# Rotary embedding in an attention slot: one 128-partition sine product with its halves swapped by SBUF transfers, and q and k projected two slots ahead

## The chip, the cores and the metric

The kernel runs on one core of one Trainium2 chip. Its time is device microseconds; three runs gave 617.77, 617.89 and 618.55 us, median 617.89. One further execution was taken with a profile. The engines are named as in the profile: PE (TensorE), with PEld for its weight loads, DVE (VectorE), ACT (ScalarE), POOL (GpSimd) and SP (SyncE, which issues all transfers of this kernel).

## What is computed

Two layers on x of 2 x 512 x 256, each an attention part and a feed-forward part, with norms between. The change touches the attention of the first layer only. Cut to what matters:

```python
D_MODEL, N_HEADS, D_K = 256, 16, 128

def rope(x):                                  # x: batch, position, head, 128
    cos, sin = ...                            # by position and frequency
    x_rot = concatenate([-x[..., 64:], x[..., :64]], axis=-1)
    return x * cos + x_rot * sin

q = rope((x @ wq.T + bq).reshape(b, s, N_HEADS, D_K))
k = rope((x @ wk.T + bk).reshape(b, s, N_HEADS, D_K))
v = (x @ wv.T + bv).reshape(b, s, N_HEADS, D_K)
attn = softmax(where(causal, -inf, einsum('bihd,bjhd->bhij', q, k) / sqrt(D_K)))
o = einsum('bhij,bjhd->bihd', attn, v).reshape(b, s, N_HEADS * D_K)
out = o @ wo.T + bo + residual
```

Then follow a feed-forward part with four-bit weights (gelu), a linear attention, and a feed-forward part whose weights are looked up in a table of 16 values (silu).

## The kernel before

All is float32. The first layer's attention is a loop over 32 slots (2 batches x 16 heads), `slot(i)`, with two more slots to drain. The order of every engine's instructions is the order in which the program writes them; nothing reorders them later. Two helpers record each instruction, which is why most rows of the profile bear the same line: L183 for DVE, ACT and POOL, L165 for transfers, L282 for matmuls. A matmul of 128 output rows is written as two of 64 rows (`halved`).

Head dimension lies on the partitions: q and k of a head are tiles of 128 x 512 (head dimension x positions). `projection(kind, i)` (L874) makes one of them. Two input chunks are multiplied into a PSUM bank `ps_mm`. Then the rotation: `a = (ps + bias) * cos`, for q as one DVE instruction, for k as an ACT instruction that adds the bias and a POOL product with cos. The half-swapped part is made straight into place by two DVE products of 64 partitions each, from the high half of PSUM to the low half of `r` and the other way (L913, L916). At the end POOL adds, `to = a + r` (L924), and the tile is qT or kT. The tiles `ra` (a) and `rr` (r) come from the pool `qk` with two buffers per tag, taken in turn by q and k; Tq and Tk also had two buffers each.

In slot i the program writes, in this order:

1. scores of head i (L1184 to L1212): PE, on the banks ps_s and ps_t. Into parts of these banks, which no score matmul starts, ACT has copied a piece of the mask a slot earlier (`prepare`, L993). DVE adds the mask and takes minima (`p<-ps_s,mask`, `mn`), ACT takes the exponentials with their sums.
2. `catch_up()`: one step of dequantising four-bit weights, if there is one: a cast on ACT, five DVE bit operations, or one DVE product of 128 x 1024. New weights are asked for in even slots from 2 on (`dequantised`, three transfers on SP), so bit operations fall into odd slots' middle and the product to their end.
3. `look_up(1)`: one of 32 terms of a table look-up: DVE writes `scratch`, POOL adds it into `wg`.
4. projections of q and k of head i+1, with the rotation; between the two, DVE's reciprocal of the sums, `rs`. Both ends `a + r` follow on POOL.
5. ACT multiplies the four blocks of p by rs.
6. PE: the output projection of head i-2 (`ps_o<-wo,oT`), then attention times v of head i-1 (`ps_t<-pT,v`), after which ACT prepares the next mask copies and evacuates oT.
7. DVE transposes the four blocks of p in 32 x 32 pieces (`turned`), and SP issues four transfers that bring them to the tile `pT` (one buffer), which step 6 of the next slot reads.
8. PE: values of a later group (`ps_mm<-wv,xTv`), evacuated by ACT; steps of norm chains that are due (`poll`); another catch_up.

The banks are taken in turn per tag (`bank`): ps_mm has two, used by q, k and v.

A small planner (`Times`, `Engine`) keeps modelled start and end times of what is written. It decides where to put `fills`: pieces of another table look-up on DVE, from slot 17 on, written when the model sees DVE waiting. The model knows tiles by the name of each allocation.

Of the kernel before, what the change touches and what calls it, by code (L numbers as in the profile page):

```python
# [10 lines left out]
F32 = mybir.dt.float32  # L11
# [5 lines left out]
AF = mybir.ActivationFunctionType  # L17
ALU = mybir.AluOpType

P = 128  # L20
HALF = P // 2
B = 2
S = 512
D = 256
NT = S // P
NK = D // P
# [15 lines left out]
NEG = -1e30  # L42
SWAPPED = (1, 2)
WARM = 9
REST = INTER - (NO - 1) * P


# [53 lines left out]
class Engine:  # L101
# [48 lines left out]
    def __getattr__(self, name):  # L150
        write = getattr(self.engine, name)

        def written(*args, **more):
            out = args[0] if args else more["out"]
            outs = [a for a in (out, more.get("accum_out")) if Times.on_chip(a)]
            ins = [
                a
                for a in (*args[1:], *(a for k, a in more.items() if k not in ("out", "accum_out")))
                if Times.on_chip(a)
            ]  # L160
            start = self.times.start(self.who, outs, ins)
            if name == "dma_start":
                self.busy = max(self.busy, start) + (0.8 if len(outs) + len(ins) == 2 else 0.45)
                self.times.add("DMA", self.busy + 3.4, outs, ins)
                return write(*args, **more)  # L165
            if self.fills and not self.filling:
                self.fill(start - 0.1)
            start = max(start, self.busy)
            psum = any("PS" in str(a.space) for a in (*outs, *ins))
            if self.other and not psum and name in Engine.HELD:  # L170
                for a, b in self.other.spans:
                    if a <= start < b:
                        start = b
            kind = dict(more)
            if name == "activation":
                kind["func"] = args[2]
            if ALU.pow in args:
                kind["pow"] = True
            n = max(math.prod(a.shape[1:]) for a in (*outs, *ins))
            self.busy = start + self.cost(name, n, kind, psum)  # L180
            self.spans.append((start, self.busy))
            self.times.add(self.who, self.busy, outs, ins)
            return write(*args, **more)  # L183

        return written
# [5 lines left out]
def sandwich_kernel(  # L191
# [26 lines left out]
    nc = tc.nc  # L218
# [10 lines left out]
    vector, scalar = Engine("DVE", nc.vector, times), Engine("ACT", nc.scalar, times)  # L229
    pool, sync = Engine("POOL", nc.gpsimd, times), Engine("SP", nc.sync, times)  # L230
# [3 lines left out]
    def bank(tag):  # L234
        tile = psum.tile([P, 512], F32, tag=tag, name=f"ps_{tag}")
        used = banks.setdefault(tag, deque(maxlen=2))
        if len(used) == 2:
            times.floor[tile.name] = times.end(used[0])
        used.append(tile.name)
        return tile  # L240
# [36 lines left out]
    def matmul(out, lhsT, rhs, start, stop, beside=False, **more):  # L277
        m = lhsT.shape[-1]
        step = HALF if halved[0] else P
        for at in range(0, m, step):  # L280
            part = slice(at, min(at + step, m))
            nc.tensor.matmul(out[part], lhsT=lhsT[:, part], rhs=rhs, start=start, stop=stop, **more)  # L282
        now[0] = max(now[0], times.start("PE", [out], [lhsT, rhs]))
        if not beside:
            now[0] += (math.prod(rhs.shape[1:]) / 0.6 + 5) / 1e3
        times.add("PE", now[0], [out], [lhsT, rhs])
# [19 lines left out]
    cos_sb = const.tile([P, S], F32, name="cos_sb")  # L306
    sin_sb = const.tile([P, S], F32, name="sin_sb")
# [9 lines left out]
    FULL = NO - 1  # L317
    wg = w1.tile([P, NK, FULL * P + 64 + REST], F32, name="wg")
    wu = w1.tile([P, NK, FULL * P], F32, name="wu")
# [17 lines left out]
    def chunk(t, kc):  # L337

        return t[:, :, kc].rearrange("p a j t -> p j a t")
# [193 lines left out]
    with ExitStack() as at:  # L533
        wp = at.enter_context(tc.tile_pool(name="wp", bufs=2))
        vp = at.enter_context(tc.tile_pool(name="vp", bufs=2))
        qk = at.enter_context(tc.tile_pool(name="qk", bufs=2))
# [40 lines left out]
        def warm_up(n):  # L577
            for _ in range(n):
                nc.tensor.matmul(warm[:, :P], lhsT=units, rhs=units, start=True, stop=True)  # L579

        warm_up(WARM)

# [4 lines left out]
        xT0 = [  # L587
            ac.tile([P, NK, S] if b == 0 else [P, 4, NK, NT, 32], F32, name=f"xT0_{b}") for b in range(B)
        ]
# [256 lines left out]
        for u in range(NU):  # L846
            for src, sc, name, to in ((gate_p, gate_s, "g", wg_u), (up_p, up_s, "u", wu_u)):
                w = fw.tile([P, 2, UNIT], F32, name=f"w{name}{u}")
                jobs.append((src, sc, u, name, w))
                to.append(w)  # L850
        for u in range(NU):
            w = fw.tile([P, 2, UNIT], F32, name=f"wd{u}")
# [9 lines left out]
        NS = B * NH  # L862
        qT, kT, vs, pT, ps_p, yb = {}, {}, {}, {}, {}, {}
# [10 lines left out]
        def projection(kind, i, tag="mm"):  # L874


            b, h = divmod(i, NH)
            gg, hh = divmod(i, HG)
            w = wts[kind, gg]
            bias = col(kind, h)  # L880
            a = qk.tile([P, S], F32, tag="ra", name="ra")
            r = qk.tile([P, S], F32, tag="rr", name="rr")
            to = qk.tile([P, S], F32, tag=f"T{kind}", name=f"{kind}T")
            lo, hi = slice(0, 64), slice(64, 128)


            for cs in [slice(0, TU), slice(TU, S)] if i == 0 else [slice(0, S)]:
                ps = bank(tag)
                first_half = i == 0 and cs.start == 0
                tiles = [slice(0, P), slice(P, TU)] if first_half and kind == "q" else [cs]  # L890
                for n, (ts, kc) in enumerate((ts, kc) for ts in tiles for kc in range(NK)):
                    matmul(
                        ps[:, ts],
                        w[:, hh, kc, :],
                        chunk(xT0[b], kc) if b else xT0[b][:, kc, ts],
                        kc == 0,
                        kc == NK - 1,
                    )
                    if first_half and (kind, n) in (("q", 1), ("k", 0)):
                        yield  # L900
                yield
                def by_scalar():
                    scalar.activation(a[:, cs], ps[:, cs], AF.Identity, bias=bias)
                    pool.tensor_mul(a[:, cs], a[:, cs], cos_sb[:, cs])


                if i and (kind == "k") == (i > 1):
                    by_scalar()
                elif not first_half:
                    vector.scalar_tensor_tensor(  # L910
                        a[:, cs], ps[:, cs], bias, cos_sb[:, cs], ALU.add, ALU.mult
                    )
                vector.scalar_tensor_tensor(  # L913
                    r[lo, cs], ps[hi, cs], bias[hi], sin_sb[hi, cs], ALU.add, ALU.mult
                )
                vector.scalar_tensor_tensor(  # L916
                    r[hi, cs], ps[lo, cs], bias[lo], sin_sb[lo, cs], ALU.add, ALU.mult
                )
                if first_half:
                    by_scalar()  # L920
            yield
            if (kind, i) == ("k", 1):
                inverted(0)
            (pool if i > 1 or kind == "q" else vector).tensor_add(to, a, r)  # L924
            (qT if kind == "q" else kT)[i] = to
# [215 lines left out]
        begun = {}  # L1141

        def started(kind, i):
            work = projection(kind, i)
            next(work)
            return work


        def slot(i):
            b, h = divmod(i, NH)  # L1150
# [65 lines left out]
            else:  # L1216
                assert not terms
            turning = []
            for kind in "qk":
                if kind == "q" and i in (0, 2, 3):  # L1220
                    pass
                elif i + 1 < NS:
                    turning.append(begun.pop((kind, i + 1), None) or started(kind, i + 1))
                    next(turning[-1])
                elif i <= NS:
                    next(main)
                    next(main)
                if kind == "q" and jobs and i % 2 == 0 and i >= 2:
                    dequantised(*jobs.popleft())
                if kind == "q" and i and now_in:  # L1230
                    inverted(i)
            for work in turning:
                next(work, None)
            if now_in:
                p, _ = ps_p[i]
                for it in reversed(range(NT)):
                    pi = p[:, p_at[it] : p_at[it] + (it + 1) * P]
                    scalar.mul(pi, pi, rs[i][:, it : it + 1])
# [37 lines left out]
        for rows, cs, base in (  # L1276
# [5 lines left out]
                out=mask[rows, cs],  # L1282
                in_=mask[rows, cs],
# [19 lines left out]
        main = ffn_hidden(0)  # L1303
# [122 lines left out]
    def silu_hidden(u):  # L1426
# [12 lines left out]
        for o in range(0, NO, 2):  # L1439
# [15 lines left out]
            else:  # L1455
# [3 lines left out]
                vector.tensor_mul(  # L1459
                    hT[:REST, o + 1, :], si[:REST, TU:], pg[64 : 64 + REST, TU:]  # L1460
                )
# [177 lines left out]
```

## Time and profile before

| what | value |
|---|---|
| median of three runs | 617.89 us |
| profiled execution, span | 616.7 us (616.669) |
| one attention slot, scores to scores (173.96 to 184.94 to 195.92) | 10.98 us |
| the same two slots, DVE busy | 9.60 and 8.23 us |
| the same two slots, ACT busy; POOL busy | 7.11 and 6.59; 5.54 and 5.54 us |
| the same two slots, mean busy share of the 16 DMA engines | 0.51 and 0.67 |
| from 600 to 610 us, and from 610 to the end: PE busy | 10.00 of 10.00, and 2.00 of 6.60 us |

Attention takes the first 350 us or so of the span; the feed-forward parts and the linear attention fill the rest. The span is from the first instruction to the last. An odd slot such as the one from 173.96 carries a step of dequantising, the even one after it does not. Columns of the timeline lines below: start and duration in us, engine, line, operation, output<-inputs, shape, number of instructions merged into the line, and in brackets the idle time of the engine ahead of it with what ended it. Pages of waits name a releaser that is inferred from semaphores.

Of the transfers the page says, with size each and median us from issue to landing:

```profile
pT<-turned SPq DMA_DIRECT2D x128, 208.0 KB, 3.9
wq<-in_wq SPq DMA_DIRECT2D x15, 256.0 KB, 4.2
sc_g<-in_gate_s SPq DMA_DIRECT2D x8, 128.0 KB, 4.2
```

SP's own timeline over one slot's pT transfers and the loads behind them:

```profile
184.22 3.17 SPq L165 DMA_DIRECT2D pT<-turned  x4
187.43 0.59 SPq L165 DMA_DIRECT2D wv<-in_wv  x1
188.07 1.12 SPq L165 DMA_DIRECT2D wo<-in_wo  x1
189.30 0.38 SPq L165 DMA_DIRECT2D pk_u<-in_up_p  x1
189.78 1.50 SPq L165 DMA_DIRECT2D sc_u<-in_up_s  x2
```

### The profile page before, as it was taken

To read this page: it belongs to the slowest core of one execution; us is meant where nothing else is said; L and a number is where in the kernel's file an instruction comes from. 1 tells how busy PE (TensorE), PEld (TensorE's weight loads), DVE (VectorE), ACT (ScalarE), POOL (GpSimd) and SP (SyncE) were. 2 spreads that over 40 slices of the span, in tenths; PEclk is the share of its full clock that TensorE was granted. 3 is DMA by queue.
4 is the path that set the end of the run, shared out by engine and by line. 5 is a ranking of instruction groups with operands and counts; after the bars stand their busy time and mean duration, and the time that the engine had idled before them with its cause. 6 is when DMAs were issued, how large, how long until landed. Compare 5 with 4: busy or idle time off the path is not lost.

```text
span 616.7 us, 13347 instructions
## 1 busy us (share of the span) xinstructions
PE 611.1 (99%) x4968; PEld 470.2 (76%) x4968; DVE 486.2 (79%) x1169; ACT 309.3 (50%) x716; POOL 277.1 (45%) x346
## 2 busy tenths in 40 slices
PE   9999999999999999999999999999999999999996
PEld 7455556566676776767777899999999999996665
DVE  7989988887887999989899789869986751562963
ACT  6657776775666657676566651232324223325210
POOL 5355657454453575855667300350261350161531
PEclk9999999999999999999999999999999999999999
DMA  8477474765647547556552340211001000001010
GB/s 228 137 186 211 107 199 125 171 168 144 158 127 177 168 116 191 152 142 178 113 141 60 84 104 26 98 35 35 1 8 31 1 18 18 1 2 35 19 53 18
DMA packets 44463, 61.43 MB, mean 100 GB/s; under 512 B 5232, under 2 KB 32368, under 8 KB 44400
## 3 DMA queue, kind: packets, MB, share of 16 engines
q1 hardware_dynamic: 44400, 60.59, 38.0%
q8 instruction: 39, 0.64, 0.4%
q14 instruction: 24, 0.20, 0.1%
HBM read 28.59 MB, written 1.05 MB: 48 GB/s over the span
## 4 chain that ended last, share of the span: by engine, by line
PE 98%; DVE 1%; issue 0%; POOL 0%; DVEq 0%
PE ps_mm L282 40%; PE ps_o L282 22%; PE ps_s L282 21%; PE ps_t L282 14%; PE ps_o L579 1%; DVE x L183 0%; DVE p L183 0%; DVE rr L183 0%; DVE ra L183 0%; DVE centred L183 0%; POOL rstd L183 0%; DVE wg L183 0%; PE ps_t L289 0%; DVE st L183 0%; DVE st_last L183 0%
## 5 line engine op out<-in xcount | busy, mean ns | idle before, releaser
L183 DVE SCALAR_TENSOR_TENSOR rr<-ps_mm,cols_sb,sin_sb 64x512 f32<-64x512 f32 (+1 forms) x126 | 93.4, 741 | 3.6 <-PE ps_mm L282 0.7
L183 POOL TENSOR_TENSOR wg<-wg,scratch 128x752 f32<-128x752 f32 x30 | 53.8, 1794 | 89.3 <-DVE scratch L183 86.9
L282 PE MATMUL ps_mm<-xT,wg 128*64 128x256 f32 (+1 forms) x704 | 89.4, 379 | 0.0
L282 PE MATMUL ps_s<-xT,wu 128*64 128x256 f32 x672 | 85.4, 379 | 0.0
L183 ACT ACTIVATE p<-p,mn 128x512 f32<-128x512 f32 (+3 forms) x128 | 70.3, 550 | 27.6 <-DVE mn L183 27.6
L282 PE MATMUL ps_o<-wd,hT 128*64 128x256 f32 (+1 forms) x704 | 77.2, 375 | 0.0
L282 PE MATMUL ps_t<-pT,v 128*64 128x256 f32 (+3 forms) x512 | 76.1, 432 | 0.0
L282 PEld LDWEIGHTS ps_mm<-xT,wg 128*64 128x64 f32 (+1 forms) x704 | 71.7, 137 | 5.5 <-ACT si L183 0.4
L282 PEld LDWEIGHTS ps_o<-wd,hT 128*64 128x64 f32 x704 | 68.9, 137 | 6.2
L282 PEld LDWEIGHTS ps_s<-xT,wu 128*64 128x64 f32 x672 | 69.5, 137 | 4.5 <-DVE hT L183 0.3
L282 PEld LDWEIGHTS ps_t<-pT,v 128*64 128x64 f32 x512 | 49.7, 137 | 27.1 <-issue 19.0
L183 ACT ACTIVATE p<-p,rs 128x512 f32<-128x512 f32 (+3 forms) x128 | 61.4, 551 | 11.2 <-DVE rs L183 9.3
L282 PEld LDWEIGHTS ps_o<-wo,oT 128*64 128x64 f32 x512 | 49.9, 137 | 17.8 <-issue 13.3
L282 PE MATMUL ps_o<-wo,oT 128*64 128x256 f32 x512 | 62.5, 379 | 0.0
L282 PE MATMUL ps_mm<-xT,wq 128*64 128x512 f32 (+2 forms) x256 | 60.5, 577 | 0.1
L282 PE MATMUL ps_mm<-xT,wk 128*64 128x512 f32 x248 | 60.0, 592 | 0.0
L183 POOL TENSOR_TENSOR ra<-ra,cos_sb 128x512 f32<-128x512 f32 (+1 forms) x33 | 41.1, 1245 | 40.2 <-ACT ra L183 38.4
L282 PE MATMUL ps_s<-kT,qT 128*64 128x64 f32 (+5 forms) x384 | 57.0, 424 | 0.0
L282 PE MATMUL ps_mm<-wv,xTv 128*64 128x256 f32 x464 | 56.4, 379 | 0.0
L183 DVE STREAM_TRANSPOSE turned<-p 128x512 f32<-128x512 f32 (+3 forms) x128 | 54.1, 480 | 1.2 <-ACT p L183 0.2
L183 ACT ACTIVATE ln<-x,shift,rstd 128x256 f32<-128x256 f32 x22 | 13.3, 607 | 79.0 <-POOL shift L183 78.2
L282 PEld LDWEIGHTS ps_s<-kT,qT 128*64 128x64 f32 x384 | 34.6, 137 | 23.9 <-issue 11.6
(161 smaller groups left out, 965.3 us busy)
## 6 DMA issues: line engine op xcount, KB each, us to landing
pT<-turned SPq DMA_DIRECT2D x128, 208.0 KB, 3.9
wo<-in_wo SPq DMA_DIRECT2D x17, 256.0 KB, 4.2
wv<-in_wv SPq DMA_DIRECT2D x16, 256.0 KB, 4.2
wq<-in_wq SPq DMA_DIRECT2D x15, 256.0 KB, 4.2
wk<-in_wk SPq DMA_DIRECT2D x15, 256.0 KB, 4.0
xT<-tr SPq DMA_DIRECT2D x48, 64.0 KB, 2.1
pk_g<-in_gate_p SPq DMA_DIRECT2D x4, 256.0 KB, 4.6
sc_g<-in_gate_s SPq DMA_DIRECT2D x8, 128.0 KB, 4.2
```

What stands on the lines that cost most here:

```text
L183: return write(*args, **more)
L282: nc.tensor.matmul(out[part], lhsT=lhsT[:, part], rhs=rhs, start=start, stop=stop, **more)
L579: nc.tensor.matmul(warm[:, :P], lhsT=units, rhs=units, start=True, stop=True)
```

## The change

From head 5 on (`FROM`) the rotation is written in another way. The sine product becomes one DVE instruction of 128 partitions into a new tile `y`, and SP swaps its halves into `r` by two transfers of 64 partitions. q and k of head i+2 are projected, rotated and swapped in slot i, instead of those of head i+1; the final sum `a + r` of head i+1 is written in slot i just before. The tiles Tq and Tk get a third buffer; `ra`, `rr` and the new `ry` have two. Slot 3 projects both head 4 and head 5. In slots 30 and 31, where no head is left, pieces of the first feed-forward part (`main`) take the place of projections. The planner's rule for transfers changes: a transfer is taken to wait for its inputs, and for earlier transfers into its output. The program is built with a smaller scratch area for transfers (1024).

```diff
+FROM = 5
...
             if name == "dma_start":
+                start = max(self.times.start(self.who, [], ins), self.times.start("DMA", outs, []))
...
-            to = qk.tile([P, S], F32, tag=f"T{kind}", name=f"{kind}T")
+            to = qk.tile([P, S], F32, tag=f"T{kind}", name=f"{kind}T", bufs=3)
             lo, hi = slice(0, 64), slice(64, 128)
+
+            if i >= FROM:
+                ps = bank(tag)
+                for kc in range(NK):
+                    matmul(
+                        ps,
+                        w[:, hh, kc, :],
+                        chunk(xT0[b], kc) if b else xT0[b][:, kc, :],
+                        kc == 0,
+                        kc == NK - 1,
+                    )
+                yield
+                y = qk.tile([P, S], F32, tag="ry", name="ry")
+                if kind == "q":
+                    vector.scalar_tensor_tensor(a, ps, bias, cos_sb, ALU.add, ALU.mult)
+                else:
+                    scalar.activation(a, ps, AF.Identity, bias=bias)
+                    pool.tensor_mul(a, a, cos_sb)
+                vector.scalar_tensor_tensor(y, ps, bias, sin_sb, ALU.add, ALU.mult)
+                for half, other in ((lo, hi), (hi, lo)):
+                    sync.dma_start(out=r[half], in_=y[other])
+                yield
+                pool.tensor_add(to, a, r)
+                (qT if kind == "q" else kT)[i] = to
+                return
...
             turning = []
+            if FROM <= i + 1 < NS:
+                for kind in "qk":
+                    next(begun.pop((kind, i + 1)), None)
             for kind in "qk":
                 if kind == "q" and i in (0, 2, 3):
                     pass
+                elif i + 1 >= FROM:
+                    if i + 2 < NS:
+                        begun[kind, i + 2] = started(kind, i + 2)
+                        next(begun[kind, i + 2])
+                    elif i <= NS:
+                        next(main)
+                        if i + 2 > NS:
+                            next(main)
...
             for work in turning:
                 next(work, None)
+            if i == FROM - 2:
+                for kind in "qk":
+                    begun[kind, FROM] = started(kind, FROM)
+                    next(begun[kind, FROM])
...
-    nc = bacc.Bacc("TRN2", target_bir_lowering=False, num_devices=1)
+    nc = bacc.Bacc("TRN2", target_bir_lowering=False, num_devices=1, dynamic_dma_scratch_size=1024)
```

The constants of the kernel: NS = 32 slots, NK = 2 input chunks, P = 128 partitions, S = 512 positions; `begun` holds projections that are under way, `started` makes one and runs its matmuls, each further `next` runs it to its next `yield`.

## The prediction, made before the changed kernel was run

> **What bounds the kernel now.** I read the busy shares first, then the granted clock by slices, then the chain of work that ended last.
>
> ```profile
> PE 611.1 (99%) x4968; PEld 470.2 (76%) x4968; DVE 486.2 (79%) x1169; ACT 309.3 (50%) x716; POOL 277.1 (45%) x346
> ...
> PEclk9999999999999999999999999999999999999999
> ...
> PE 98%; DVE 1%; issue 0%; POOL 0%; DVEq 0%
> ```
>
> TensorE holds 99% of the span, at full clock, and 98% of the last chain. "Busy" can hide waiting, so I looked at the order of time in one attention slot (slot 15, an odd one), TensorE first:
>
> ```profile
> 173.96 1.78 PE L282 MATMUL ps_s<-kT,qT 128*64 128x512 f32 x12
> ...
> 181.06 2.38 PE L282 MATMUL ps_t<-pT,v 128*64 128x512 f32 x16
> ...
> 184.94 0.60 PE L282 MATMUL ps_s<-kT,qT 128*64 128x512 f32 x2
> ```
>
> The slot lasts 10.98 us from scores to scores, and so does the next (184.94 to 195.92), though VectorE has 9.60 us of work in the one and 8.23 in the other (busy time by stage). A period that ignores VectorE's load is TensorE's own work. So in attention nothing outside TensorE sets the time, and taking work from VectorE can gain almost nothing: the change adds and removes no matmul, and 616.67 - 611.1 = 5.6 us of TensorE idleness lies at the two ends (0.76 before the first matmul, 4.6 in the last 6.6). What can move is upwards only: how close are the other engines to making TensorE wait? VectorE, GpSimd and ScalarE in slot 15:
>
> ```profile
> 177.87 0.61 DVE L183 TENSOR_SCALAR scratch<-scratch,lut_sb 128x752 f32<-128x752 int32 x1
> 178.39 0.75 DVE L183 SCALAR_TENSOR_TENSOR ra<-ps_mm,cols_sb,cos_sb 128x512 f32<-128x512 f32 x1
> 179.15 1.51 DVE L183 SCALAR_TENSOR_TENSOR rr<-ps_mm,cols_sb,sin_sb 64x512 f32<-64x512 f32 x2
> 180.70 0.18 DVE L183 RECIPROCAL rs<-sm 128x4 f32<-128x4 f32 x1
> 180.91 1.51 DVE L183 SCALAR_TENSOR_TENSOR rr<-ps_mm,cols_sb,sin_sb 64x512 f32<-64x512 f32 x2
> 182.46 1.69 DVE L183 STREAM_TRANSPOSE turned<-p 128x512 f32<-128x512 f32 x4
> ```
>
> ```profile
> 178.56 1.79 POOL L183 TENSOR_TENSOR wg<-wg,scratch 128x752 f32<-128x752 f32 x1 [5.35 <-DVE scratch L183]
> 180.44 1.28 POOL L183 TENSOR_TENSOR ra<-ra,cos_sb 128x512 f32<-128x512 f32 x1
> 181.67 1.28 POOL L183 TENSOR_TENSOR qT<-ra,rr 128x512 f32<-128x512 f32 x1
> 182.91 1.28 POOL L183 TENSOR_TENSOR kT<-ra,rr 128x512 f32<-128x512 f32 x1
> ```
>
> ```profile
> 179.67 0.69 ACT L183 ACTIVATE ra<-ps_mm,cols_sb 128x512 f32<-128x512 f32 x1 [1.52 <-PE ps_mm L282]
> 180.91 1.92 ACT L183 ACTIVATE p<-p,rs 128x512 f32<-128x512 f32 x4 [0.55 <-DVE rs L183]
> 182.86 0.21 ACT L183 COPY ps_s<-mask 64x64 f32<-64x64 f32 x1
> ```
>
> The reader is to see three things. The copy of the mask into ps_s ends at 183.07; the scores at 184.94 need it, so it has 1.87 us to spare. GpSimd sits idle 5.35 us until the look-up product `scratch` is ready, then does wg, ra, qT, kT; kT ends 0.75 us before its scores. And the transposes end at 184.15; their four transfers to pT take 3.17 us to issue and the last lands near 190.85, against TensorE's use of pT at 192.03: 1.2 us to spare.
>
> **The change part by part.** Below, t is time from the slot's first score matmul (173.96 is t = 0).
>
> *Sine products.* Two 64x512 products of 0.75 us become one 128x512. Its nearest row is the cosine product, 128x512 from the same bank, 0.75. So VectorE is rid of 2 x 0.76 = 1.5 us a slot, 27 heads (5 to 31), some 41 us in all. On the path: nothing, TensorE covers it.
>
> *Swap by transfers.* Four more transfers of 128 KB a slot on SP's queue. They land in time: a 64-partition 128 KB transfer (sc_g) takes 4.2 us to land, so q's, issued by 8.9, are there at 13.1 and k's, issued by 12.1 at the latest, at 16.3; the sums that need them come in the next slot, after t = 17 and 18. [...]
>
> *The wait that is added.* The final sum of head i+1 (`to = a + r` on GpSimd) is now issued in slot i's middle, behind the look-up sum wg, and right after it the cosine product of head i+2 is written. Tiles "ra" have two buffers for q and k in turn, so q of head i+2 takes the buffer that q of head i+1 is still to be read from. VectorE's `ra` for q must wait for GpSimd's qT sum, ScalarE's `ra` for k for its kT sum. Before, the buffers were read a slot earlier, and these sums came after all of it. Behind VectorE's wait stand y of q, rs, y of k and the four transposes (and with them pT); behind ScalarE's stand the four p products, the mask copies, oT and v.
>
> Odd slot with look-up and dequantising (7 to 25 but 17, and 5: ten slots): scratch ends at t = 4.52, wg 4.60 to 6.39, qT to 7.67, kT to 8.91 (sums start 1.24 apart), ScalarE's ra +0.06 and 0.69 to 9.66, the p products 1.92 to 11.58, the copy 0.03 + 0.21 to 11.82, and 0.08 until the scores start: 11.90, against 10.98. Late by 0.92. Hand-overs of 0.03 to 0.08 are those seen between engines in these rows. Ten slots: 9.2, and with 0.03 of lag in each slot that follows (below), 9.5 us.
>
> Even slot: scratch ends at 3.46 (188.40), all the rest alike: 10.84. No wait, but 0.14 of margin.
>
> *VectorE's lag into the next slot.* In the odd slot VectorE starts ra at 7.73, y(q) ends 9.24, y(k) waits for ScalarE's ra and ends 10.47, transposes 12.20, the dequantised weights (1.20, 1.12 of it after the transposes' recorded end) 13.24. The next slot's score reductions could start at 11.90 + 1.17 = 13.07. So any further work at the end of an odd slot makes the next slot late by about its length, since idle time spent in the new wait cannot be used by what is queued behind. From the rows (statistics 0.42, aggregate 0.18, add 0.52, transpose 0.43, h sum 0.68) this is 1.40 in slot 5, 0.85 in 7, 2.24 in 19, 0.85 in 21, 2.24 in 23, 0.85 in 25: 8.4. Ends of even slots (1.26 in slot 4, 1.2 in 18 and 22, with a fill of 0.43 in each of the latter two) exceed their 1.09 of room and give 1.25; the second look-ups of slots 26 to 29 some 0.9. Together 10.6. At the low end these are hidden (0), if the norm work lands where GpSimd makes VectorE wait anyway.
>
> *SP's queue.* In even slots up to 22 the packed weights and scales (0.38 + 1.50 to 2.4 us of issue; I take 2.0) stand between q's swap and k's. q's y ends at t = 8.18, two issues of 0.6 (the 256 KB loads' row, 0.59; pT's own transfers take 0.55 to 1.17) to 9.45, weights to 11.45, k's to 12.65: only then can pT go, instead of 11.2. Its last landing, 6.63 after its first issue, is t = 19.28; TensorE wants it at 10.98 + 7.10 = 18.08. The odd slot that follows stops 1.2 at pT and lasts 8.30 + 3.88 = 12.18 instead of 11.90. Ten slots x 0.28 = 2.8, less where slots are longer anyway: 2.5 us. If the last landing takes 8.2 (the worst in this trace after the transposes, median 6.7), every slot stops there and the whole becomes 35 to 38; if SP keeps up, 0.
>
> Sum: 9.5 + 10.6 + 2.5 = 22.6 us on the profiled 616.67, that is 639.3. The runs' median, 617.89, lies 1.22 above the profiled span; with that, 640.5.
>
> *Third buffers for qT and kT, less scratch for DMA, the two earlier projections in slot 3, feed-forward pieces in slots 30 and 31.* The same matmuls in another place; TensorE's count is unchanged and the pieces moved cover the same dependent work. Nothing; if a piece of cover is missed there, one slot's wait, about 1 us.
>
> *Clock.* It is 1.00 in all stages but the last 6.6 us, where TensorE works 2.0 us and it reads 0.84. My waits are at most 2.4 us in a slot of 11 to 13, so I count nothing. [...]
>
> **Rivals.**
> *Not slower: the wait is covered.* If GpSimd's sums ran before the look-up sum is ready (q's operands have landed by t = 2.1), VectorE would not wait, transposes end 1.5 us earlier than now, and every slot stays 10.98: 617.9. It decides at t = 4.0: the qT sum must end before that. Against it: the code issues the look-up before the sums, and each engine's rows follow issue order. Chance 0.05; a gain over 0.2% has nothing to come from but the idle ends: 0.01 of it.
> *Chain alone.* The wait is there, but the lag at the slots' ends is absorbed: 9.5 to 14, so 627 to 632. For it: VectorE has 1.5 us less to do. Chance 0.17.
> *pT becomes the bound.* 4 x 128 KB a slot more on engines that are 0.51 to 0.67 busy there, ahead of pT in the queue: landing 7.7 to 8.2 gives 30 to 38, so 648 to 656. For it: landings up to 8.2 occur already. Against: the median is 6.7 with the present load. Chance 0.2.
>
> **How the numbers follow.** Forecast (632 to 648, most likely 640.5) 0.55; chain alone 0.17; pT bound 0.2; covered 0.05; further out 0.03. Range 626 to 656, from the chain alone to the late landing. A measurement of this kernel can tell about 0.2% (1.2 us) from no change: slower 0.95, same 0.04, faster 0.01.
>
> **What would show it.** Right: in the profile after, VectorE's `ra` stands idle some 3 us on GpSimd's qT; ScalarE's `ra` on kT; score matmuls wait on ScalarE's mask copy; slots alternate near 11 and 12 us; sine products of 128x512 at 0.75. Wrong: slots still 10.98 (the wait is covered), TensorE waiting at ps_t for pT in every slot (the transfers bound it), or a clock below 1.00 in attention.

## The result, and the profile after

The changed kernel takes 643.56 us (median of 4 runs, 643.17 to 644.24), the kernel before beside it 618.22 (617.77 to 618.7): a ratio of 1.0413, 95% interval 1.0398 to 1.0428. The forecast was 640.5, in a range of 626 to 656. The profiled execution has a span of 642.3 us, 25.6 more than the 616.67 before.

First the busy shares, TensorE's row of the slices and the chain of the changed kernel's page, as before (the helpers' lines are now L185, L167 and L284):

```profile
span 642.3 us, 13490 instructions
PE 616.1 (96%) x4968; PEld 397.1 (62%) x4968; DVE 436.9 (68%) x1115; ACT 304.8 (47%) x716; POOL 276.0 (43%) x346
...
PE   9999899999999998899799999999999999999996
...
PE 54%; issue 17%; POOL 13%; ACT 5%; DMA 4%; DVE 4%; SPq 2%; POOLq 0%; DVEq 0%
```

VectorE is rid of 49 us (486.2 before): by its groups 40.7 of them are the sine products (93.4 before, 40.3 + 12.4 after). But the chain of waits, which was TensorE to 98%, is TensorE to 54% now; GpSimd has 13% of it. Where they meet is in the view of waits (engine, tile and line, what ended the idle time, us in all, times, longest):

```profile
ACT ra L185 <- POOL kT L185: 104.1, 27, 4.7
...
DVE ra L185 <- POOL qT L185: 78.3, 25, 3.2
...
PE ps_t L284 <- DMA pT<-turned: 16.3, 13, 2.2
...
PE ps_s L284 <- ACT ps_s L185: 1.7, 3, 0.6
```

The two rows of `ra` are new; the kernel before has neither wait. VectorE stands 3.1 us in each of 25 slots, and ScalarE 3.9 in each of 27, in front of a product into `ra` until GpSimd has made a final sum. But the rows of TensorE, the engine that counts, say that what it waits for last is mostly not ScalarE's copy of the mask (1.7 us) but pT's transfers (16.3). Slot 15, engine by engine (start, duration, the operation, the idle time before it and its releaser; the slot's scores start at 188.51, and t counts from the start of a slot's scores, as in the forecast):

```profile
192.46 0.60 DVE L185 TENSOR_SCALAR scratch<-scratch,lut_sb 128x752 f32<-128x752 int32 x1
196.18 0.75 DVE L185 SCALAR_TENSOR_TENSOR ra<-ps_mm,cols_sb,cos_sb 128x512 f32<-128x512 f32 x1 [3.12 <-POOL qT L185]
```

```profile
193.14 1.78 POOL L185 TENSOR_TENSOR wg<-wg,scratch 128x752 f32<-128x752 f32 x1 [5.71 <-DVE scratch L185]
194.88 1.27 POOL L185 TENSOR_TENSOR qT<-ra,rr 128x512 f32<-128x512 f32 x1
196.10 1.27 POOL L185 TENSOR_TENSOR kT<-ra,rr 128x512 f32<-128x512 f32 x1
```

```profile
197.41 0.69 ACT L185 ACTIVATE ra<-ps_mm,cols_sb 128x512 f32<-128x512 f32 x1 [4.67 <-POOL kT L185]
...
199.93 0.21 ACT L185 COPY ps_s<-mask 64x64 f32<-64x64 f32 x1
```

```profile
187.45 1.21 SPq L167 DMA_DIRECT2D sc_g<-in_gate_s  x2
188.77 1.17 SPq L167 DMA_DIRECT2D rr<-ry  x2
190.04 3.44 SPq L167 DMA_DIRECT2D pT<-turned  x4
```

```profile
197.16 2.37 PE L284 MATMUL ps_t<-pT,v 128*64 128x512 f32 x16 [1.36 <-DMA pT<-turned]
...
201.06 1.33 PE L284 MATMUL ps_s<-kT,qT 128*64 128x448 f32 x6
```

The reader can follow one string: the look-up product ends at 193.06, GpSimd's wg 194.92, its qT 196.15, and 0.03 later VectorE starts `ra`; its kT ends at 197.37, and 0.04 later ScalarE starts. The copy of the mask ends at 200.14, t = 11.63 where 11.82 was forecast. Yet the scores start only at t = 12.55, because TensorE had been stopped earlier, at the product with pT: SP had the packed weights and k's swap ahead of pT's transfers in slot 14, and the last of these lands at 197.02. So the mask is in time, and the forecast's third term, pT behind SP's queue, is the one TensorE sees.

Adding up by TensorE's own starts what each slot lasts above 10.98 us: stops at ps_t 19.7 us (17.8 of them in the eleven odd slots 5 to 25, the rest in 10, 20, 27, 28 and 29), scores late for the copy 2.4 (slots 20, 23, 24), a bank for v 1.0 (slot 24), slot 3 1.1, and 1.7 in slot 5, after whose stop of 2.44 us TensorE ran for 3.41 us at half clock (last section). Together 25.9, against 25.6 in the span; as the first scores come 0.7 us earlier than in the kernel before (13.71 against 14.41), some 26.3 had to be found, so 0.4 is without a place.

### The profile page after: what moved, and what is told of

Same layout as the page of the kernel before. It is cut to its first block, busy times and chain, and to the rows that moved or that the text cites. A ratio compares the mean times of both kernels' runs of the same rounds, so it can differ in the third digit from the quotient of the medians.

```text
span 642.3 us, 13490 instructions
## 1 busy us (share of the span) xinstructions
PE 616.1 (96%) x4968; PEld 397.1 (62%) x4968; DVE 436.9 (68%) x1115; ACT 304.8 (47%) x716; POOL 276.0 (43%) x346
## 4 chain that ended last, share of the span: by engine, by line
PE 54%; issue 17%; POOL 13%; ACT 5%; DMA 4%; DVE 4%; SPq 2%; POOLq 0%; DVEq 0%
PE ps_mm L284 19%; PE ps_s L284 15%; PE ps_o L284 15%; PE ps_t L284 5%; POOL kT L185 4%; POOL qT L185 4%; DMA pT<-turned 3%; POOL ra L185 2%; ACT ra L185 2%; SPq L167 2%; ACT p L185 2%; DVE turned L185 1%; POOL rstd L185 1%; POOL wg L185 1%; POOL shift L185 1%
## 5 line engine op out<-in xcount | busy, mean ns | idle before, releaser
L185 POOL TENSOR_TENSOR wg<-wg,scratch 128x752 f32<-128x752 f32 x30 | 53.6, 1788 | 103.1 <-DVE scratch L185 100.6
L284 PE MATMUL ps_t<-pT,v 128*64 128x256 f32 (+3 forms) x512 | 76.5, 440 | 16.5 <-DMA pT<-turned 16.3
L284 PE MATMUL ps_mm<-xT,wg 128*64 128x256 f32 x704 | 86.0, 379 | 0.0
L284 PE MATMUL ps_s<-xT,wu 128*64 128x256 f32 x672 | 82.1, 379 | 0.0
L185 ACT ACTIVATE p<-p,mn 128x512 f32<-128x512 f32 (+3 forms) x128 | 70.3, 551 | 24.0 <-DVE mn L185 23.9
L185 DVE SCALAR_TENSOR_TENSOR ra<-ps_mm,cols_sb,cos_sb 128x512 f32<-128x512 f32 (+1 forms) x32 | 23.6, 739 | 78.4 <-POOL qT L185 78.3
L284 PE MATMUL ps_o<-wd,hT 128*64 128x256 f32 (+1 forms) x704 | 76.7, 375 | 0.0
L284 PEld LDWEIGHTS ps_t<-pT,v 128*64 128x64 f32 x512 | 40.6, 138 | 56.8 <-issue 43.5
L185 ACT ACTIVATE ra<-ps_mm,cols_sb 128x512 f32<-128x512 f32 (+1 forms) x31 | 21.0, 678 | 104.1 <-POOL kT L185 104.1
L284 PEld LDWEIGHTS ps_mm<-xT,wg 128*64 128x64 f32 x704 | 55.8, 137 | 19.9 <-ACT si L185 0.4
L284 PEld LDWEIGHTS ps_o<-wd,hT 128*64 128x64 f32 x704 | 55.1, 137 | 19.8
L284 PEld LDWEIGHTS ps_s<-xT,wu 128*64 128x64 f32 x672 | 53.5, 137 | 19.0 <-DVE hT L185 0.3
L185 ACT ACTIVATE p<-p,rs 128x512 f32<-128x512 f32 (+3 forms) x128 | 61.1, 550 | 2.4 <-DVE rs L185 2.4
L284 PE MATMUL ps_o<-wo,oT 128*64 128x256 f32 x512 | 61.2, 379 | 0.0
L284 PE MATMUL ps_mm<-xT,wk 128*64 128x512 f32 x248 | 59.0, 592 | 0.9 <-DVE rr L185 0.9
L284 PE MATMUL ps_mm<-xT,wq 128*64 128x512 f32 (+2 forms) x256 | 59.5, 577 | 0.1
L284 PE MATMUL ps_s<-kT,qT 128*64 128x448 f32 (+5 forms) x384 | 57.8, 425 | 1.7 <-ACT ps_s L185 1.7
L284 PEld LDWEIGHTS ps_o<-wo,oT 128*64 128x64 f32 x512 | 41.2, 137 | 26.0 <-issue 14.8
L284 PE MATMUL ps_mm<-wv,xTv 128*64 128x256 f32 x464 | 56.3, 383 | 0.8 <-DVE rs L185 0.8
L185 POOL TENSOR_TENSOR ra<-ra,cos_sb 128x512 f32<-128x512 f32 (+1 forms) x33 | 41.2, 1249 | 33.6 <-ACT ra L185 33.6
L185 DVE STREAM_TRANSPOSE turned<-p 128x512 f32<-128x512 f32 (+3 forms) x128 | 53.8, 476 | 1.5 <-ACT ps_s L185 1.3
L284 PEld LDWEIGHTS ps_s<-kT,qT 128*64 128x64 f32 x384 | 37.0, 137 | 23.6 <-issue 9.9
```

## Experiments

Twelve kernels, each a small edit of the changed kernel (one of the kernel before). All medians stand beside the kernel before in the same sessions, 618.0 to 618.2 us.

| run | edit | us | ratio to before, 95% interval |
|---|---|---|---|
| changed kernel | | 643.56 | 1.0413 (1.0398 to 1.0428) |
| e1 | sums ahead of the look-up sum | 622.52 | 1.0072 (1.0055 to 1.0089) |
| e2 | third buffers for ra and rr | 622.61 | 1.0072 (1.0057 to 1.0087) |
| e3 | packed weights behind pT | 713.62 | 1.1545 (1.1527 to 1.1563) |
| e4 | two products, no swaps | 674.01 | 1.0905 (1.0888 to 1.0922) |
| e5 | packed weights ahead of the swaps | 638.99 | 1.0333 (1.0317 to 1.0348) |
| e6 | third buffer for ra alone | 626.33 | 1.0138 (1.0116 to 1.0159) |
| e7 | swaps, one slot ahead | 706.39 | 1.1443 (1.1412 to 1.1473) |
| e8 | e1, each swap twice | 749.55 | 1.2132 (1.2092 to 1.2173) |
| e9 | e1, swaps and as many spare transfers | 649.48 | 1.0513 (1.0487 to 1.0539) |
| e10 | e1, two products, no swaps | 625.41 | 1.0120 (1.0106 to 1.0134) |
| e11 | e1, e2 and e5 together | 622.96 | 1.0081 (1.0067 to 1.0094) |
| e12 | e2 and e5 together | 622.64 | 1.0067 (1.0053 to 1.0080) |

### e1: the order on GpSimd

```diff
+            if FROM <= i + 1 < NS:
+                for kind in "qk":
+                    next(begun.pop((kind, i + 1)), None)
             catch_up()
             if i < NS - 2:
                 look_up(i > 0)
...
-            if FROM <= i + 1 < NS:
-                for kind in "qk":
-                    next(begun.pop((kind, i + 1)), None)
```

> The changed kernel with one thing moved: GpSimd's final sums of head i+1 are written ahead of the look-up work of slot i, so GpSimd does qT, kT, ra, wg instead of wg, qT, kT, ra. Theory (the order on GpSimd is the root: the product into ra waits behind qT's sum, which stands behind wg): the idle time of VectorE ahead of ra on qT falls from 78 us to under 10, slots go back to about 10.98 us, 617 to 621 us. Rival A (the transfers are the cause, because pT stands behind the swaps in SP's queue): VectorE no longer waits but TensorE still waits at ps_t for pT, 630 us or more. Rival B (the work moved into slots 3, 30 and 31 costs): 643 stays.

622.52 us, 1.5 above the theory's range: 21.0 of the 25.3 us are gone by three lines that change places. Rival B is out, and A as well: no transfer was taken away, and pT is in time in all but two slots. GpSimd and VectorE in slot 15, whose scores start at 177.82 here:

```profile
175.93 1.27 POOL L185 TENSOR_TENSOR qT<-ra,rr 128x512 f32<-128x512 f32 x1 [1.36 <-DMA rr<-ry]
179.51 1.28 POOL L185 TENSOR_TENSOR kT<-ra,rr 128x512 f32<-128x512 f32 x1 [2.31 <-DMA rr<-ry]
182.43 1.79 POOL L185 TENSOR_TENSOR wg<-wg,scratch 128x752 f32<-128x752 f32 x1 [1.64 <-DVE scratch L185]
```

```profile
181.75 0.60 DVE L185 TENSOR_SCALAR scratch<-scratch,lut_sb 128x752 f32<-128x752 int32 x1
182.27 0.74 DVE L185 SCALAR_TENSOR_TENSOR ra<-ps_mm,cols_sb,cos_sb 128x512 f32<-128x512 f32 x1
```

GpSimd used the time in which it stood idle for the look-up product (5.71 us in the changed kernel): it now waits for the swaps to land, and is done with both sums at t = 2.97, ahead of the point, t = 4.0, that the forecast's first rival named. VectorE starts `ra` with no wait. All slots from 4 to 29 are 10.98, but 20 and 23 (0.28 and 0.46 at pT). What is left is 4.35 us by the medians and 3.75 by the profiled spans. In the profile it is 1.10 in slot 3, 0.74 in these two, and 2.7 in three stops in the feed-forward part, before the matmuls that start at 413, 423 and 439 us (on ScalarE's ge, a transfer of xT, and VectorE's hT), which the changed kernel and e2 don't show and e11 does; the first scores start 0.7 us earlier than in the kernel before. Why the earlier sums lead there was not followed up.

### e2 and e6: the buffers

```diff
-            a = qk.tile([P, S], F32, tag="ra", name="ra")
-            r = qk.tile([P, S], F32, tag="rr", name="rr")
+            a = qk.tile([P, S], F32, tag="ra", name="ra", bufs=3)
+            r = qk.tile([P, S], F32, tag="rr", name="rr", bufs=3)
```

e6 has the first of these two lines only.

> The changed kernel with three buffers instead of two for ra and rr, the order of all work untouched. The product into ra then waits for a sum that is a slot older. Theory (it is the reuse of two buffers that turns GpSimd's order into a wait): waits of ra on qT and kT near 0, 617 to 622 us. Rival (late sums hurt in themselves, the scores or the swap being late on them): stays above 635 us with TensorE waiting for kT.

> The changed kernel with a third buffer for ra alone; rr keeps two, so the swap transfers of q and k still wait in SP's queue for GpSimd's sums, and pT behind them. Theory (the loss is the wait of VectorE and ScalarE, and SP's own wait ends at t = 7.7 and 8.9, when y is hardly done anyway): 620 to 627 us. Rival (the wait in SP's queue alone keeps pT late): 632 us or more.

622.61 (0.6 above the theory's range) and 626.33 (inside it): the order is as in the changed kernel, the look-up first and the sums late, and the loss is gone all the same, so late sums don't hurt in themselves. One thing was expected wrongly. With three buffers taken in turn by q and k, only q's product finds a buffer that was read a slot earlier; k's gets the one that the same slot's qT sum reads. ScalarE and VectorE in slot 15 of e2 (scores at 179.65):

```profile
184.10 0.75 DVE L185 SCALAR_TENSOR_TENSOR ra<-ps_mm,cols_sb,cos_sb 128x512 f32<-128x512 f32 x1
```

```profile
187.31 0.69 ACT L185 ACTIVATE ra<-ps_mm,cols_sb 128x512 f32<-128x512 f32 x1 [3.45 <-POOL qT L185]
...
189.83 0.21 ACT L185 COPY ps_s<-mask 64x64 f32<-64x64 f32 x1
```

ScalarE still waits 3.45 us, 68.3 us over the span, one sum less than before; its copy ends at t = 10.39, 0.6 before the scores. A wait of that length is free as long as it ends in time: the same row in the view of waits, 104 us in the changed kernel and 68 here, stands beside 21 us of difference. e6 shows that 3.7 of them come from SP: with two buffers of rr, the swap transfers wait for the sums in SP's queue, with pT behind them (TensorE stops at ps_t in 12 slots, 0.3 to 2.0 us each).

### e3 and e5: pT's place in SP's queue

```diff
-                if kind == "q" and jobs and i % 2 == 0 and i >= 2:
-                    dequantised(*jobs.popleft())
...
             if now_in:
                 turned_p(i)
+            if jobs and i % 2 == 0 and i >= 2:
+                dequantised(*jobs.popleft())
```

> The changed kernel with the transfers of packed weights and scales (even slots) moved behind pT's in SP's queue; the wait on GpSimd's sums is left in. Theory (GpSimd's wait 20 us, the weights standing ahead of pT a smaller part): odd slots then are limited by the copy of the mask, near 11.9 instead of 12.6 us, ten slots, so 5 to 8 us less: 635 to 639 us. Rival A (the queue is all of it): 617 to 622. Rival B (pT is late only because the transposes are late, the queue costs nothing): 642 to 644.

713.62, none of the three. The move made a new wait. ScalarE's cast of the packed weights stands in its queue ahead of the exponentials of the odd slot; slot 15 (scores at 223.77), ScalarE and then TensorE:

```profile
231.23 0.62 ACT L185 CAST p<-pk_g 128x512 uint8<-128x512 int32 x1 [6.45 <-DMA pk_g<-in_gate_p]
```

```profile
238.21 3.68 PE L284 MATMUL ps_mm<-wv,xTv 128*64 128x256 f32 x16 [5.00 <-DVE rs L185]
```

The weights, issued at 227.19 behind pT, land 4.0 us later, all softmax work of the slot stands behind them, and TensorE stops for 5.2 to 5.8 us in every odd slot from 3 to 25 but 17 (2.4). So the run says nothing on the question that it was made for, and it was asked again with the weights put where SP is idle, ahead of both swaps:

```diff
             turning = []
...
+            if jobs and i % 2 == 0 and i >= 2:
+                dequantised(*jobs.popleft())
             for kind in "qk":
...
-                if kind == "q" and jobs and i % 2 == 0 and i >= 2:
-                    dequantised(*jobs.popleft())
```

> The changed kernel with the transfers of packed weights and scales (even slots) issued ahead of both swaps instead of between them; SP stands idle there, so they delay nothing, and pT goes some 1.2 to 1.8 us earlier. GpSimd's wait is left in. Theory (the wait on the sums is 20 us of the loss and pT's place in SP's queue the rest): odd slots are then limited by the copy of the mask, 11.9 instead of 12.3 to 12.9 us, 635 to 639 us. Rival A (pT's lateness is all): 617 to 622. Rival B (pT is late only through the transposes): 642 to 644.

638.99: 4.6 us less than the changed kernel, at the upper edge of the theory's range. And now, in slot 15 and in the others like it (7, 13, 21), the wait that the forecast had named is the one TensorE sees. Slot 15 (scores at 186.55), ScalarE and TensorE:

```profile
197.99 0.21 ACT L185 COPY ps_s<-mask 64x64 f32<-64x64 f32 x1
```

```profile
193.66 2.34 PE L284 MATMUL ps_t<-pT,v 128*64 128x512 f32 x16
...
198.35 1.08 PE L284 MATMUL ps_s<-kT,qT 128*64 128x448 f32 x4 [0.60 <-ACT ps_s L185]
```

No stop at ps_t, and the scores start at t = 11.80 (forecast 11.90) behind the copy, which ends at 198.20. Over the whole of e5 both waits are left: its view of waits has 5.6 us of TensorE's idle time on the copy of the mask and 6.7 on pT. Slot lengths by TensorE's starts:

| slot | changed kernel | e5 weights first | e1 sums first |
|---|---|---|---|
| 7 | 12.25 | 11.81 | 10.98 |
| 13 | 12.64 | 11.79 | 10.98 |
| 15 | 12.55 | 11.79 | 10.98 |
| 17 (no dequantising) | 12.37 | 11.02 | 10.98 |
| 21 | 12.88 | 11.81 | 10.98 |

### e4 and e10: what the single product is worth

```diff
-                y = qk.tile([P, S], F32, tag="ry", name="ry")
...
-                vector.scalar_tensor_tensor(y, ps, bias, sin_sb, ALU.add, ALU.mult)
                 for half, other in ((lo, hi), (hi, lo)):
-                    sync.dma_start(out=r[half], in_=y[other])
+                    vector.scalar_tensor_tensor(
+                        r[half], ps[other], bias[other], sin_sb[other], ALU.add, ALU.mult
+                    )
```

e4 is the changed kernel with this edit, e10 is e1 with it.

> The changed kernel's order and its two-slots-ahead projection, but with the sine part as two products of 64 partitions as before and no swap transfers. Theory (the added wait is the cause): it is not undone; VectorE has 1.5 us a slot more behind its wait, transposes and pT come later, but pT has fewer transfers ahead of it: 640 to 660 us. Rival (swap transfers are the cause): back towards 618, under 628 us.

> The kernel with the sums ahead of the look-up work, the sine part as two products of 64 partitions, no swap transfers. It shows what the single product is worth where nothing waits for GpSimd. Theory (nothing: TensorE covers VectorE's 41 us): 618 to 623 us, within 2 us of the same kernel with swaps (622.5). Rival (VectorE's time counts behind the earlier projection): 627 us or more.

Without the transfers e4 is 30.5 us slower, not faster, so the swaps are not the cause. The theory had the sign and too small a size (640 to 660; 674.01 came): behind the wait VectorE's 1.5 us a slot count in even slots as well, which last 12.15 to 13.8 us from 6 to 28, but for slot 18 (11.4). With the wait gone (e10) the same edit costs 2.9 us (625.41 against 622.52), between the two answers that were expected. So the product's saving on VectorE is real, but its worth in time depends on what VectorE stands behind: 30 us in the changed kernel, which the change itself put there, and 3 where nothing waits; and the kernel before, two products and one slot ahead, has 618.

### e7: one slot ahead

e7 is the kernel before with the lines below (heads before 5 keep the two products), and with the planner's rule for transfers and the smaller scratch area of the change.

```diff
-                vector.scalar_tensor_tensor(
-                    r[lo, cs], ps[hi, cs], bias[hi], sin_sb[hi, cs], ALU.add, ALU.mult
-                )
...
+                if i >= FROM:
+                    y = qk.tile([P, S], F32, tag="ry", name="ry")
+                    vector.scalar_tensor_tensor(y, ps, bias, sin_sb, ALU.add, ALU.mult)
+                    for half, other in ((lo, hi), (hi, lo)):
+                        sync.dma_start(out=r[half], in_=y[other])
```

> The kernel before with the sine part as one product of 128 partitions and swap transfers from head 5 on, but q and k still projected one slot ahead of their scores. Theory: the sum of k now waits for k's swap, which in even slots stands behind the packed weights, and the scores wait for it: even slots 2 to 3 us longer, odd ones up to 0.5, 640 to 665 us; VectorE doesn't wait for GpSimd. Rival (swaps land in time one slot ahead also): 617 to 622 us.

706.39, worse than expected, by the mechanism that was expected. GpSimd and TensorE at the end of slot 14:

```profile
205.64 1.26 POOL L185 TENSOR_TENSOR kT<-ra,rr 128x512 f32<-128x512 f32 x1 [3.29 <-DMA rr<-ry]
```

```profile
206.96 3.25 PE L284 MATMUL ps_s<-kT,qT 128*64 128x448 f32 x11 [4.05 <-POOL kT L185]
```

The scores wait 3 to 5.5 us for k's swap in the even slots up to 24, and here then take 3.25 us in place of 1.7: TensorE is at half clock, for 51.2 us in this run, which is worth 25.6; 681 would be left. So with SP's queue as it is laid out, swaps by transfers need the second slot of lead, and the wait for the sums is what that brought.

### e8 and e9: more transfers

```diff
+                spare = qk.tile([P, S], F32, tag="spare", name="spare")
+                for half, other in ((lo, hi), (hi, lo)):
+                    sync.dma_start(out=spare[half], in_=y[other])
```

e9 is e1 with this behind the two swaps of each projection; e8, run first, sent the second pair into r itself.

> The kernel with the sums ahead of the look-up work, with every swap transfer issued twice (eight of 128 KB a slot instead of four). Theory (swap transfers cost nothing while SP's queue has room; four more cost 2.4 us of issue ahead of pT, whose margin is then used up): 625 to 645 us, TensorE waiting at ps_t for pT. Rival (room is left): under 624 us.

> The kernel with the sums ahead of the look-up work, and with each swap transfer followed by a second one of the same bytes into a tile that nobody reads, so that only room in SP's queue and on the DMA engines is taken and no transfer waits for another's landing, as they did where both wrote the same place. Theory (the swaps cost nothing as long as pT still lands in time; its margin there is 1.5 to 1.9 us by the landings, and four more issues of 0.55 to 0.6 take 2.4): TensorE waits 0.5 to 1 us at ps_t in most slots, 632 to 648 us. Rival (margin is left): under 625 us. [...]

e8 (749.55) answers another question: writing the same place twice, the second pair of transfers waits in SP's queue for the first to land, and pT behind it (here the first pair lands at 246.72 and 246.94, and the next issue starts at 247.10).

```profile
242.43 9.31 SPq L167 DMA_DIRECT2D rr<-ry  x8
```

Eight issues last 9.31 us; e9's eight, with no landing to wait for, take some 5.0. e9 gives 649.48, a little over the theory's range: TensorE stops 0.9 to 2.5 us at ps_t in the odd slots from 5 to 25, 2 to 3 us in slots 10, 22 and 26 and under 0.6 in the other even ones, and behind two of these stops (slots 10 and 19) it ran at half clock, which cost 3.3 us in all. The transfers of e1, which e9 was made from, and then of e9, from their pages (KB each, median us from issue to landing):

```profile
pT<-turned SPq DMA_DIRECT2D x128, 208.0 KB, 3.9
rr<-ry SPq DMA_DIRECT2D x108, 128.0 KB, 2.6
```

```profile
pT<-turned SPq DMA_DIRECT2D x128, 208.0 KB, 4.0
rr<-ry SPq DMA_DIRECT2D x108, 128.0 KB, 3.7
spare<-ry SPq DMA_DIRECT2D x108, 128.0 KB, 3.2
```

Twice the transfers slow the swaps (2.6 to 3.7 us) but hardly pT's landing (3.9 before the change, 3.9 in e1, 4.0 here). So by these medians what more transfers cost pT is their place ahead of it in the queue, not room on the DMA engines.

### e11 and e12: the repairs together

> The changed kernel with all three repairs at once: sums ahead of the look-up work, third buffers for ra and rr, packed weights ahead of the swaps. Theory (attention is then TensorE's own work again, and the work moved into slot 3 costs 1.1 us): 618.5 to 621 us, slots of 10.98, not faster than before. Rival (VectorE's saved time then shows): under 616.5 us.

> The changed kernel with third buffers for ra and rr and the packed weights ahead of the swaps, the sums still behind the look-up sum: the second run above without its remaining waits for pT (3.6 us), and without the 2.7 us of waits in the feed-forward part that only the kernels with sums first show. Theory (nothing is left but the 1.1 us of slot 3): 618.5 to 620.5 us. Rival A (pT is late through the transposes, which still come after ScalarE's wait): 621 to 624. Rival B (VectorE's saved time is worth something after all): under 616.5.

622.96 and 622.64, both above the theories' ranges and no better than one repair alone. In e11 attention's slots are 10.98 but for 3, 20 and 23, and its loss is that of e1: 1.6 in slot 3, 1.6 at pT, 2.6 in the feed-forward part. In e12's profile pT is late in slots 6, 11, 20 and 23, most where SP had four transfers of xT as well ahead of the swaps in the slot before (2.2 us in slot 11, with 1.75 lost at half clock behind it, 1.7 in slot 23). That profile is of the slowest of the five runs (625.64), and by the mean clocks the only one with such a stretch at half clock. The median lies between rival A's bounds, from another cause than it named. No version here is faster than the kernel before, and none could be expected to be: its TensorE has no gap in attention that these edits could close.

## Why the prediction held, step by step

*TensorE is full, nothing to gain.* Right: with VectorE at 449 us (e11) or 495.8 (e10), attention's slots are at best 10.98.

*The wait for the sums.* Right in place, order and time: taken away in two independent ways (e1 by order, e2 by buffers) it gives back 21 us, together with the lag and the lateness of pT that hung on it. GpSimd's sums end at t = 7.64 and 8.86 (forecast 7.67 and 8.91), the copy of the mask at 11.63 (11.82). Its term, 0.92 an odd slot, came out at 0.82, as e5 shows in slots 7, 13, 15 and 21.

*VectorE's lag, 10.6.* About right in sum, and in part by luck. e5 has it without the weights ahead of pT: its slots add up to 20.9 us above 10.98; less slot 3 (1.2) and ten times 0.82, 11.5 are left, in slots 5, 6, 10, 11, 19, 20, 23, 24 and 27 mostly. The places are not the forecast's: the six slots behind the odd ends that it named (6, 8, 20, 22, 24, 26) hold 5.5 where it had 8.4, the three behind the even ends (5, 19, 23) 3.0 where it had 1.25, and slots 10, 11 and 16, which it did not name, 1.9. Nor is the way: the forecast had the next slot's softmax work late, but by TensorE's starts some 11 of e5's 20.9 us are stops at ps_t and some 8 at the scores. That each microsecond of it is due to the work named was not tried one by one.

*SP's queue, 2.5.* Right in kind, and somewhat low: e5 gives back 4.6 by the medians. Part of that is the half clock behind pT's stop in slot 5, 1.7 in the profiled execution; but only two of the changed kernel's four runs have the mean clock (0.997) that goes with it, and against the other two (0.999; 643.17 and 643.18) e5 gives back 4.2. So the queue's share lies between 2.9 and 4.2. In its parts it was off too. The forecast had pT's first issue at t = 12.65 and the last landing at 19.28; slot 14 measured 12.52 and 19.50, with 0.14 more until the matmul. So TensorE stops 1.57 us in slot 15, not 1.2, and the scores come at 12.55, not 12.18. Slot 17 pays 1.4 too, though it was left out of the ten. In return a longer odd slot hides VectorE's lag behind it: e5's even slots 6, 8, 10, 16 and 22 last 11.4 to 12.3 us, the changed kernel's 10.98, but for slot 10 (11.58). What was wrong is the place in the list of signs: the list of what would be seen had TensorE waiting for the mask in most slots, and it is pT that is later in nearly all of them, though the forecast's own sum had priced pT as the later one (12.18 against 11.90).

*Swap transfers land in time and cost nothing.* Right on landing (2.4 us at the median, where 4.2 was taken from the nearest row). In the changed kernel q's pair of swaps in the odd slot 13 landed 0.68 us apart, 2.25 and 2.37 us after issues that were 0.56 apart; so the second came at most 0.12 us later than its later issue explains. What they do cost is their time in SP's queue, part of the term above.

*Third buffers, moved projections: nothing, or one wait of 1 us.* The wait is there, in slot 3, 1.1 us: the third projection of that slot needs a bank that VectorE's sine products of head 4 still read.

*Clock: nothing.* Wrong by 1.7 us in the profiled execution, once, in slot 5, behind a stop of 2.44 us; two of the four runs seem to be without it. That waits of at most 2.4 us leave the clock at 1.00 was the author's estimate. The trace of the kernel before does not show it: the longest gap between TensorE's recorded matmuls in attention is 0.10 us there.

By the profiled spans the sum came out 3.0 us low (639.3 against 642.3), and the two items priced at nothing, the clock (1.7) and slot 3 (1.1), are 2.8 of it; that so little else is left is partly because errors of place inside the terms cancel. The median, 3.1 above the forecast, lies 1.3 above the profiled span, where 1.22 was taken. Of the rivals, "pT becomes the bound" had the place right and the reason wrong: from first issue to last landing pT takes 6.7 us before and after alike (medians over the slots whose landings are recorded, 12 before and 5 after); it is issued late.

## What to carry to other kernels

Before a value is made earlier, look at which engine reads its buffer last and what stands ahead of that read in that engine's queue: two buffers and one look-up product ahead of the sums turned a sum that its own reader could still wait for into the head of VectorE's, ScalarE's and SP's queues. Time taken from an engine that isn't the bound is worth little until something makes that engine wait (2.9 us of some 41 in e10), and then most of its length (30 in e4); so price a saving and the waits that come with it in the same slot, not apart. And a transfer on a shared queue is priced by what stands behind it: against their place ahead of the swaps, the packed weights cost 4.6 us more between them and 75 more behind pT (part of both at half clock).

## What the runs showed that was not expected

TensorE's clock fell to half after some stops of little over 2 us. In slot 5 of the changed kernel (the stretch in us, its length, busy time and count of each engine, the granted clock of TensorE, the share of the DMA engines, GB/s):

```profile
76.00:78.00 2.00, 0.47 (x3) 0.24 (x5) 1.07 (x2) 0.00 (x0) 2.00 (x2) 1.00 0.88 283
78.00:80.00 2.00, 2.00 (x12) 1.12 (x10) 1.55 (x4) 1.84 (x4) 1.20 (x2) 0.68 0.27 67
80.00:82.00 2.00, 2.00 (x15) 1.49 (x13) 1.93 (x9) 1.76 (x5) 0.20 (x1) 0.50 0.96 204
```

The stop, 2.44 us by TensorE's starts and 2.23 between its recorded matmuls, ends at 77.5; the clock falls at 78.72, while TensorE is at work again, and stays at 0.50 for 3.41 us. All periods of half clock in the attention parts of these traces last 3.41 us or two or three times that, and within one execution they all start on one grid of 3.41 us. Laying that grid over the traces that have such periods (after, e3, e4, e7, e8, e9, e12), with TensorE's idle time taken from the end of one recorded matmul to the start of the next, a cell at full clock is followed by one at half clock when TensorE was idle for 2.01 us or more of it (40 cells, all of them), and not when it was idle for 2.00 us or less (711 cells); as the ends are modelled, the bound is near 2 us, not exact. So in these runs one stop of 2.0 to 3.7 us between recorded matmuls did or did not cost some 1.7 us more (half of 3.41), by how the grid cut it (12 of 20 such stops did; all 28 over 4 us). In e3, e7 and e8 it comes to 65, 51 and 82 us at half clock, worth 32, 26 and 41 us of their time, which is part of why these three came out so far above what was expected. The forecast's "nothing" for waits of up to 2.4 us does not hold in them: the shortest stop with a fall behind it is 2.01 us between recorded matmuls (e12, slot 11).
